# A frequency convolution whose odd chunk pairs hold their two halves swapped

## The chip, the core and the metric

The kernel runs on one core of a Trainium2 chip. The core has five engines that run at the same time and wait for each other through semaphores: TensorE (PE, matrix products), VectorE (DVE), ScalarE (ACT), GpSimd (POOL), and SyncE (SP, which here only issues DMA transfers). TensorE is an array of 128 x 128 cells. A product whose contraction has at most 64 rows, or whose result has at most 64 partitions, uses only a part of the array, and products on different parts can run side by side. Results of products go to PSUM, which has eight banks of 512 float32 per partition. Everything here is float32.

The metric is the device time of one execution in microseconds (us), lower is better.

## The reference, cut to what matters

The input x is (4, 512, 128, 64): batch B, time T, f, h. There are two layers. Layer 0 works on D = 128 * 64 = 8192 features per time step:

```
xn = layernorm(x over D);  k = xn @ Wk;  v = xn @ Wv;  r = sigmoid(xn @ Wr)     # D_STATE = 64
s_t = decay * s_(t-1) + k_t * v_t
x  = x + (r * s) @ Wo
xn = layernorm(x over D)
fo = conv over f, three taps, mixing all 64 h:  fo[f] = sum over d in -1, 0, 1 of freq_W[d] @ xn[f + d]
x  = x + gelu(fo + freq_b)
xn = layernorm(x over D);  to = depthwise causal conv over time, three taps;  x = x + layernorm(to)
x  = x + gelu(x @ W1 + b1) @ W2 + b2                                            # per (b, t, f): 64 -> 256 -> 64
```

Layer 1 takes a moving average over time as the trend, a Fourier transform of the rest over time, mixes its 128 lowest modes by one complex matrix per h, transforms back and adds the trend. The change touches layer 0 only; layer 1 reads what layer 0 leaves in DRAM.

The convolution over f is the place of the change. With 64 h per f, a chunk of 128 partitions holds two neighbouring f. One product of 128 x 128 covers what the two f of a chunk give to themselves and to each other. What is left are the two neighbours outside the chunk: the f before its first and the f after its second. Each of these is a product of 64 x 64.

## The kernel before, in words

The features lie on the partitions and time on the free axis: 64 chunks of (128, 512), handled in 32 pairs of chunks. For each batch layer 0 has stages, each a Python generator that writes instructions and yields after each step:

- `project(b)`: k, v and r for each pair, from loads of x (`xp`), of the weights and (batches 1 to 3) of x in rows for the statistics. Its TensorE line is L327; L324 scales the weights on VectorE.
- `scan(b)`: statistics, the recurrence, the gates; a chain of small steps.
- `attend_and_convolve(b)`: for each pair, `attend` (product with Wo, L453; sum with x, L455; scaling, L459, which gives `z`), and two pairs later `convolve`, then the column sums for the next layer norm (`add_up`, L215).
- `convolve_time(b)`: the causal convolution (VectorE lines L546, L548, L555) and again `add_up`.
- `open_feed(b)` and `feed_forward(b)`: the last layer norm and the feed-forward of each chunk: `widen` (L605), ScalarE's gelu (L609), `narrow` (L616, L621), and `store`: four transposes (L630) into one bank `pt`, a ScalarE copy of it into the row tile `ob` (L634), and a store to DRAM for every fourth chunk.

Before all that stands `project(0)`, and after it `prepare()`, which convolves the layer norm's scale and shift once (L153 to L163) for use as a correction inside the convolution (`cgr`, L474).

`convolve(i)` works on a PSUM tile `cv` of two banks, one for each chunk j of the pair. It issues four small products for the correction (L474), then the neighbours' products, then one full product for each chunk (L488); gelu, the sum (L491) and a square follow on ScalarE and VectorE. The neighbours' products of a pair are four: for each chunk one from the second half of the chunk before into the first half of this one, and one from the first half of the chunk after into the second half of this one:

```
if c > 0:
    nc.tensor.matmul(cv[0:H, j, :], lhsT=ws[c - 1][H:P, P:], rhs=zs[c - 1][H:P, :], ...)      # L481
if c < NCH - 1:
    nc.tensor.matmul(cv[H:P, j, :], lhsT=ws[c + 1][0:H, P:], rhs=zs[c + 1][0:H, :], ...)      # L484
```

So all L481 contract the rows 64 to 127 into the columns 0 to 63 of the array, and all L484 the rows 0 to 63 into the columns 64 to 127. `ws[c]` are the convolution's weights times the layer norm's scale of chunk c, made by ScalarE (L467).

The order: TensorE's instructions keep the order in which the code writes them. `in_turn` runs two generators side by side and takes steps from one or the other by given shares: `scan` and `attend_and_convolve` of batch 0 beside `project` and `scan` of batch 1; then `convolve_time(0)` beside `attend_and_convolve(1)`; then `feed_forward(0)` beside `project(2)`; and so on; near the end `feed_forward(2)` beside `convolve_time(3)`, and `feed_forward(3)` alone. On the other engines and DMA queues a scheduler orders the instructions by its own estimate of when each is ready; every engine and queue then runs its list in order. Buffers come from pools with a fixed number of copies, and a new use waits for the last reader of the old one. The PSUM pools have one copy each: a (two banks), c (two), m (two), s (one), p (one).

Of the kernel before, what the change touches and what calls it, by code (L numbers as in the profile page):

```python
# [12 lines left out]
ALU = mybir.AluOpType  # L13
# [3 lines left out]
P = 128  # L17
T = 512
NF = 128
H = 64  # L20
D = NF * H
NCH = D // P
SL = 512
NS = D // SL
NPR = NCH // 2
NT = T // P
S = 64
# [3 lines left out]
HALO = KMA // 2  # L31

MODES = np.concatenate([np.arange(0, M, 2), np.arange(1, M, 2)])
EPS = 1e-5


G1, B1, G2, B2, G3, B3, TB, G4, B4, W0, W1, W2 = range(12)
# [33 lines left out]

@with_exitstack
def layer0(ctx, tc, dram, x, xt, vecs, wkvr, wo, wdec, wconv, fbias, w1, fb1, w2, fb2, x4):


    nc = tc.nc
# [17 lines left out]
    def two(pool, tag):  # L94
        return pool.tile([P, 2, SL], F32, tag=tag, name=tag)
# [48 lines left out]
    tb_all = const.tile([P, NCH], F32, name="tb_all")  # L144
    fix = const.tile([P, NCH, 2], F32, name="fix")

    def prepare():

        both = rowp.tile([P, SL], F32, tag="rg", name="both")[:, 0:P].rearrange("p (k c) -> p k c", k=2)
        pc = two(ps_c, "c")  # L150
        for k, v in ((0, G2), (1, B2)):
            o = pc[:, k, :]
            nc.tensor.matmul(o[:, 0:NCH], lhsT=wc_sb[:, 0:P], rhs=vec[:, v, :], start=True, stop=True)  # L153
            nc.tensor.matmul(
                o[0:H, 1:NCH], lhsT=wc_sb[H:P, P:], rhs=vec[H:P, v, 0 : NCH - 1], start=False, stop=True,
                skip_group_check=True,
            )
            nc.tensor.matmul(
                o[H:P, 0 : NCH - 1], lhsT=wc_sb[0:H, P:], rhs=vec[0:H, v, 1:NCH], start=False, stop=True,
                skip_group_check=True,  # L160
            )
        nc.vector.tensor_scalar_mul(both[:, 0, :], pc[:, 0, 0:NCH], -1.0)
        nc.vector.tensor_scalar(both[:, 1, :], pc[:, 1, 0:NCH], fb_sb, None, ALU.add)  # L163
        pg = two(ps_c, "c")
        nc.tensor.transpose(pg[:, 0, 0:P], both.rearrange("p k c -> p (k c)"), ident)
        cgt = rowp.tile([P, SL], F32, tag="state", name="cgt")[:, 0:P]
        nc.vector.tensor_copy(cgt, pg[:, 0, 0:P])
        for k in range(2):
            nc.scalar.dma_start(cgd[:, k, :], cgt[k * NCH : (k + 1) * NCH, :])
# [267 lines left out]
    def attend_and_convolve(b):  # L437
# [23 lines left out]
        def scaled(i):  # L461

            wcs = fr.tile([P, 2, P + H], F32, tag="wcs", name="wcs")
            for j in range(2):
                c = 2 * i + j
                ws[c] = wcs[:, j, :]
                nc.scalar.mul(wcs[:, j, :], wc_sb, vec[:, G2, c : c + 1])  # L467

        def convolve(i):
            cv = c_bank() if i % 2 or held[0] else two(ps_m, "m")  # L470
            for h in range(2):
                for j in range(2):
                    q = 32 * (2 * h + j)
                    nc.tensor.matmul(  # L474
                        cv[h * H : (h + 1) * H, j, :], lhsT=cgr[q : q + 2, i, :], rhs=mb[q : q + 2, :],
                        start=True, stop=False,
                    )
            for j in range(2):
                c = 2 * i + j
                if c > 0:  # L480
                    nc.tensor.matmul(cv[0:H, j, :], lhsT=ws[c - 1][H:P, P:], rhs=zs[c - 1][H:P, :], start=False,  # L481
                                     stop=False)
                if c < NCH - 1:
                    nc.tensor.matmul(cv[H:P, j, :], lhsT=ws[c + 1][0:H, P:], rhs=zs[c + 1][0:H, :], start=False,  # L484
                                     stop=False)
            for j in range(2):
                c = 2 * i + j
                nc.tensor.matmul(cv[:, j, :], lhsT=ws[c][:, 0:P], rhs=zs[c], start=False, stop=True)  # L488
            nc.scalar.activation(cv, cv, AF.Gelu_apprx_tanh)
            x2 = two(bk, "x2")  # L490
            nc.vector.tensor_tensor(x2, cv, x1s.pop(i), ALU.add)  # L491
            nc.gpsimd.dma_start(x2d[b][2 * i : 2 * i + 2].rearrange("c p t -> p c t"), x2)
            sq2 = bk.tile([P, 2, SL], F32, tag="sq", name="sq2")
            nc.scalar.activation(sq2, x2, AF.Square)  # L494
            for c in (2 * i - 2, 2 * i - 1):
                zs.pop(c, None)
                ws.pop(c, None)
            if i + 2 < NPR:
                scaled(i + 2)
            waiting[i] = x2, sq2  # L500
# [95 lines left out]
    def feed_forward(b):  # L596
# [28 lines left out]
        def store(c):  # L625
# [5 lines left out]
            s = c // 4  # L631
            if c % 4 == 0:
                obs[s] = bk.tile([P, NT, SL], F32, tag="ob", name="ob")
            nc.scalar.copy(obs[s][:, :, c % 4 * P : (c % 4 + 1) * P], pt)  # L634
            if c % 4 == 3:
                nc.gpsimd.dma_start(
                    x4[b][:, s * SL : (s + 1) * SL].rearrange("(t p) d -> p t d", p=P), obs.pop(s)
# [292 lines left out]
def _inputs(x, i):  # L930


    def cols(v):
        return v.reshape(NCH, P).T

    time_w = i["time_W"].reshape(D, 3)
    vecs = [i[n] for n in ("ln_attn_g", "ln_attn_b", "ln_freq_g", "ln_freq_b", "ln_time_g")]
    vecs += [i[n] for n in ("ln_time_b", "time_b", "time_ln_g", "time_ln_b")]
    vecs += [time_w[:, k] for k in range(3)]
    wkvr = np.concatenate([i["Wk"], i["Wv"], i["Wr"], i["Wo"].T], axis=1)  # L940
    wo = i["Wo"].reshape(S, NPR, 2, P).transpose(2, 0, 1, 3)
    taps = i["freq_W"].transpose(2, 1, 0)
    wconv = np.zeros((P, 3 * H), np.float32)
    for a in range(2):
        for b in range(2):
            wconv[a * H : (a + 1) * H, b * H : (b + 1) * H] = taps[a - b + 1]
    wconv[H:, 2 * H :] = taps[0]
    wconv[:H, 2 * H :] = taps[2]
    b = x.shape[0]
    a = {  # L950
        "x": x.reshape(b, T, D),
        "xt": x.reshape(b, T, D).transpose(0, 2, 1).reshape(b, NCH, P, T),
        "vecs": np.stack([cols(v) for v in vecs], axis=1),
        "wkvr": wkvr.reshape(NCH, P, 4 * S),
        "wo": wo.reshape(P, NPR, P),
        "wdec": np.concatenate([i["w_decay"]] * 2)[:, None],
        "wconv": wconv,
# [26 lines left out]
```

## Time and profile before

| what | value |
|---|---|
| time, median of 3 runs | 4107.79 us (4098.11 to 4113.56) |
| time of the profiled execution | 4118.44 us |
| its span, first to last instruction | 4116.7 us |
| TensorE busy / granted clock, mean | 3908.1 us (95%) / 0.972 |
| VectorE busy | 2493.7 us (61%) |
| ScalarE busy | 1796.8 us (44%) |
| GpSimd busy | 527.2 us (13%) |

By stage (busy us of the engines within each stretch of the span):

| stretch, us | what runs | TensorE | VectorE | ScalarE | clock | DMA GB/s |
|---|---|---|---|---|---|---|
| 0 to 186 | `project(0)` | 180.9 | 25.8 | 38.0 | 1.00 | 155 |
| 186 to 262 | `prepare`, `scan(0)`, `project(1)` | 64.8 | 36.2 | 6.5 | 0.89 | 210 |
| 262 to 583 | `attend_and_convolve(0)` beside `project(1)`, `scan(1)` | 311.8 | 162.9 | 98.4 | 0.97 | 200 |
| 583 to 873 | `convolve_time(0)` beside `attend_and_convolve(1)` | 272.9 | 267.6 | 165.0 | 0.97 | 239 |
| 873 to 1298 | `feed_forward(0)` beside `project(2)` | 413.2 | 232.0 | 226.2 | 0.98 | 215 |
| 1298 to 1586 | `convolve_time(1)` beside `attend_and_convolve(2)` | 273.7 | 269.9 | 164.0 | 0.97 | 243 |
| 1586 to 2013 | `feed_forward(1)` beside `project(3)` | 415.5 | 225.8 | 224.8 | 0.98 | 212 |
| 2013 to 2309 | `convolve_time(2)` beside `attend_and_convolve(3)` | 275.9 | 268.6 | 164.6 | 0.94 | 239 |
| 2309 to 2600 | `feed_forward(2)` beside `convolve_time(3)` | 249.9 | 278.0 | 232.1 | 0.96 | 241 |
| 2600 to 2972 | `feed_forward(3)` | 365.3 | 202.9 | 276.2 | 0.99 | 161 |
| 2972 to 4116 | layer 1 | 1084.1 | 523.9 | 201.0 | 0.97 | 207 |

How to read the profile's lines: an engine is busy while an instruction of its own runs; waits and the issue of transfers are not counted. A group of instructions is given as line, engine, operation, output <- inputs, shape and count, then the busy time of the group (overlaps counted once), the mean duration in ns, and the idle time of the engine just before such instructions with what ended it. Products overlap in TensorE's pipeline, so their mean duration is longer than their spacing, and a float32 product is recorded as two instructions. Some records of products can be missing. The clock is the share of full speed that TensorE was granted.

### The profile page before, as it was taken

The numbers are of one execution on the slowest core, as the hardware profiler recorded it, in microseconds if no ns is written. First come the engines' busy times: TensorE is split into PE (matmuls) and PEld (weight loads), VectorE is DVE, ScalarE is ACT, GpSimd is POOL, SyncE is SP. The second block draws the span as 40 slices with busy tenths as digits, with TensorE's granted clock in tenths as the row PEclk, the third lists the DMA queues.
The fourth block names the chain that finished last, engine by engine and source line by source line (L and its number), as shares of the span: only waits on it lengthen the run. The fifth ranks groups of instructions, "written<-read, shape, count | busy, mean of one in ns | idle before, by whom it ended". The sixth has DMA issues, their size and how long they took to land. (4 is left out here: it accounts for less than half of the span.)

```text
span 4116.7 us, 46561 instructions
## 1 busy us (share of the span) xinstructions
PE 3908.1 (95%) x16939; PEld 1460.7 (35%) x16939; DVE 2493.7 (61%) x3168; ACT 1796.8 (44%) x2396; POOL 527.2 (13%) x942
## 2 busy tenths in 40 slices
PE   9999989999999999999999888999899999999998
PEld 4433322233333223333322322333325733228433
DVE  1145549975556997555699899655443355542555
ACT  2112336545555554555565678777622211122111
POOL 0000012310000221000122122000032000130000
PEclk9989999999999999999999999999999999999999
DMA  5466647776664776666477676555385377882577
GB/s 170 157 209 235 208 132 250 252 246 228 238 224 152 240 258 237 222 234 231 157 249 250 217 251 238 187 168 184 133 254 168 95 258 243 272 245 72 186 241 239
DMA packets 445854, 867.80 MB, mean 211 GB/s; under 512 B 35321, under 2 KB 101561, under 8 KB 445625
## 3 DMA queue, kind: packets, MB, share of 16 engines
q1 hardware_dynamic: 347136, 588.34, 44.6%
q0 software_dynamic: 62464, 207.66, 14.4%
q10 hardware_dynamic: 36024, 68.82, 4.5%
q8 instruction: 135, 2.21, 0.2%
q14 instruction: 95, 0.77, 0.1%
HBM read 596.18 MB, written 268.50 MB: 210 GB/s over the span
## 5 line engine op out<-in xcount | busy, mean ns | idle before, releaser
L616 PE MATMUL pa<-mid,w_sb 128*64 128x512 f32 x2048 | 499.7, 609 | 43.0 <-DVE x4t L621 42.6
L609 ACT ACTIVATE mid<-m,fb_sb 128x1024 f32<-128x1024 f32 x256 | 285.0, 1113 | 303.4 <-PE m L605 303.0
L621 DVE SCALAR_TENSOR_TENSOR x4t<-pa,fb_sb,x 128x512 f32<-128x512 f32 x252 | 188.0, 746 | 263.2 <-PE pa L616 263.2
L605 PE MATMUL m<-x,w_sb 64*128 64x512 f32 x1008 | 290.8, 650 | 5.7 <-ACT mid L609 5.2
L555 DVE SCALAR_TENSOR_TENSOR to<-xh,vec,to 128x512 f32<-128x512 f32 x384 | 277.0, 744 | 12.6 <-issue 8.6
L609 ACT ACTIVATE mid<-c,fb_sb 128x1024 f32<-128x1024 f32 x256 | 283.3, 1107 | 1.4 <-PE c L605 1.2
L845 ACT COPY even<-a 128x512 f32<-128x512 f32 x128 | 71.7, 588 | 480.3 <-PE b L865 145.8
L865 PE MATMUL b<-xin,avg_sb 128*128 128x512 f32 x512 | 246.6, 626 | 35.5 <-DMA xin<-x 32.4
L605 PE MATMUL c<-x,w_sb 64*128 64x512 f32 x1008 | 264.5, 598 | 0.7 <-ACT mid L609 0.7
L616 PEld LDWEIGHTS pa<-mid,w_sb 128*64 128x64 f32 x2048 | 124.8, 136 | 387.7 <-issue 229.8
L780 DVE TENSOR_TENSOR uv<-xin 128x1024 f32<-128x1024 f32 x128 | 151.2, 1222 | 172.4 <-PE a L791 135.7
L327 PE MATMUL a<-xp,both 128*128 128x512 f32 x512 | 247.5, 610 | 6.4 <-DVE both L324 5.9
L848 DVE TENSOR_TENSOR pm<-even,a 128x512 f32<-128x512 f32 x256 | 159.3, 683 | 143.5 <-ACT even L845 109.7
L791 PE MATMUL a<-uv,dft_sb 128*64 128x512 f32 x1024 | 241.2, 612 | 0.0
L840 PE MATMUL a<-xf,idft_sb 64*128 64x512 f32 x1024 | 239.8, 602 | 0.6 <-DVE pm L848 0.4
L871 DVE TENSOR_TENSOR xin<-b,pm 128x512 f32<-128x512 f32 x256 | 159.1, 684 | 116.4 <-PE b L868 116.4
L634 ACT COPY ob<-pt 128x512 f32<-128x512 f32 x256 | 148.9, 582 | 165.5 <-PE pt L630 165.2
L324 DVE TENSOR_SCALAR both<-both,vec 128x192 f32<-128x192 f32 x192 | 53.2, 316 | 251.9 <-DMA both<-in_wkvr 220.6
L796 ACT COPY xf<-a 128x512 f32<-128x512 f32 x128 | 80.9, 632 | 266.1 <-PE a L791 266.1
L215 PE MATMUL st<-x,ones 128*32 128x512 f32 x512 | 182.4, 615 | 14.3 <-DVE x L491 14.3
L582 ACT ACTIVATE kd<-kd,vec 128x512 f32<-128x512 f32 x256 | 193.5, 809 | 4.3 <-DVE kd L574 4.2
L494 ACT ACTIVATE sq<-x 128x1024 f32<-128x1024 f32 x128 | 134.6, 1052 | 117.7 <-DVE x L491 117.4
(234 smaller groups left out, 6879.3 us busy)
## 6 DMA issues: line engine op xcount, KB each, us to landing
xp<-in_xt SPq DMA_DIRECT2D x256, 512.0 KB
xin<-x SPq DMA_DIRECT2D x128, 1024.0 KB
kx<-x SPq DMA_DIRECT2D x224, 512.0 KB
x<-x POOLq DMA_DIRECT2D x128, 512.0 KB, 4.2
kh<-to SPq DMA_DIRECT2D x128, 512.0 KB
x<-ob POOLq DMA_DIRECT2D x64, 1024.0 KB, 6.6
out<-xin ACTq DMA_DIRECT2D x64, 1024.0 KB
both<-in_x SPq DMA_DIRECT2D x96, 512.0 KB
```

Source lines behind the costliest of these rows:

```text
L215: nc.tensor.matmul(st[32 * q : 32 * q + 32, :], lhsT=ones, rhs=src[:, j, :], start=first, stop=last,)
L327: nc.tensor.matmul(pa[:, k, :], lhsT=wq[:, j, k * P : (k + 1) * P], rhs=xp[:, j, :], start=first and j == 0, stop=last and j == 1,)
L555: nc.vector.scalar_tensor_tensor(to[:, j, :], xh[:, j, k : SL + k], vec[:, w, c], to[:, j, :], ALU.mult, ALU.add)
L582: tc.keep_in_program_order(nc.scalar.activation(d[:, j, :], d[:, j, :], AF.Identity, bias=vec[:, B4, c], scale=vec[:, G4, c]))
L605: nc.tensor.matmul(pm[:, h, :], lhsT=w1_sb[hs, m * P : (m + 1) * P], rhs=x3[hs, :], start=True, stop=True)
L609: nc.scalar.activation(mid, pm, AF.Gelu_apprx_tanh, bias=fb1_sb[:, m : m + 1])
L616: nc.tensor.matmul(pa[h * H : (h + 1) * H, :], lhsT=w2_sb[:, m, :], rhs=mid[:, h, :], start=(m == 0), stop=(m == 1),)
L621: nc.vector.scalar_tensor_tensor(x4t, pa, fb2_sb, x3s[c // 2][:, c % 2, :], ALU.add, ALU.add)
L791: nc.tensor.matmul(pf[r][h * H : (h + 1) * H, :], lhsT=dft_sb[:, h, i, r, :], rhs=uv[h][:, i, :], start=False, stop=(i == 1),)
L840: nc.tensor.matmul(eo[h], lhsT=idft_sb[hs, r, i, :], rhs=xf[hs, r, c], start=(r == 0), stop=(r == 1),)
L848: nc.vector.tensor_tensor(pm[:, k, :], even, eo[1], op)
L865: nc.tensor.matmul(po[j], lhsT=avg_sb[:, j, :], rhs=xin[:, j, :], start=True, stop=False)
```

## The change

In every second pair of chunks (the odd pairs) the two f of each chunk change places: partitions 0 to 63 hold the second f and 64 to 127 the first. All that lies along the features follows on the host: the transposed x, the vectors, the projection weights, Wo. The convolution's weights exist twice, for even and for odd pairs (q = 0 and 1), and `scaled` takes the one of its pair. The neighbours' products are found by two small functions. They are still four per pair, and each falls on another quarter: for an even pair, chunk j = 0 takes both its neighbours from the rows 0 to 63 and chunk j = 1 both from the rows 64 to 127; for an odd pair it is the other way round; and the two products of a chunk go to the two column halves.

`prepare` does its small convolution by chunk number modulo 4, with results in two PSUM tiles (pools c and m) instead of one. `store` puts the halves of an odd pair's chunk back in their places: its copy out of PSUM is two copies of 64 columns per transpose instead of one of 128.

```diff
+HALVES = np.arange(D).reshape(-1, 2, 2, 2, H)
+HALVES[:, 1] = HALVES[:, 1, :, ::-1].copy()
+HALVES = HALVES.reshape(D)
...
+    halves = [slice(0, H), slice(H, P)]
+
+    def neighbours(q, c):
+
+        return (c - 1, q), (c + 1, 1 - q)
+
+    def rows_of(q, d):
+
+        return 1 - q if d < 0 else q
+
     def prepare():
...
-        pc = two(ps_c, "c")
+
+        pcs = two(ps_c, "c"), two(ps_m, "m")
         for k, v in ((0, G2), (1, B2)):
-            o = pc[:, k, :]
-            nc.tensor.matmul(o[:, 0:NCH], lhsT=wc_sb[:, 0:P], rhs=vec[:, v, :], start=True, stop=True)
-            nc.tensor.matmul(
-                o[0:H, 1:NCH], lhsT=wc_sb[H:P, P:], rhs=vec[H:P, v, 0 : NCH - 1], start=False, stop=True,
-                skip_group_check=True,
-            )
-            nc.tensor.matmul(
-                o[H:P, 0 : NCH - 1], lhsT=wc_sb[0:H, P:], rhs=vec[0:H, v, 1:NCH], start=False, stop=True,
-                skip_group_check=True,
-            )
-        nc.vector.tensor_scalar_mul(both[:, 0, :], pc[:, 0, 0:NCH], -1.0)
-        nc.vector.tensor_scalar(both[:, 1, :], pc[:, 1, 0:NCH], fb_sb, None, ALU.add)
+            for r in range(2):
+                for q in range(2):
+                    j = r if q == 0 else 1 - r
+                    o, src = pcs[r][:, k, 0:NCH], vec[:, v, :]
+                    at = slice(2 * q + j, NCH, 4)
+                    nc.tensor.matmul(
+                        o[:, at], lhsT=wc_sb[:, q, 0:P], rhs=src[:, at], start=q == 0, stop=True,
+                        skip_group_check=True,
+                    )
+                for q in range(2):
+                    j = r if q == 0 else 1 - r
+                    for d, n in neighbours(q, 0):
...
+                        nc.tensor.matmul(
+                            pcs[r][halves[n], k, first : last + 1 : 4], lhsT=wc_sb[rs, qn, P:],
+                            rhs=vec[rs, v, first + d : last + d + 1 : 4], start=False, stop=True,
+                            skip_group_check=True,
+                        )
+        for r in range(2):
+            for q in range(2):
+                at = slice(2 * q + (r if q == 0 else 1 - r), NCH, 4)
+                nc.vector.tensor_scalar_mul(both[:, 0, at], pcs[r][:, 0, at], -1.0)
+                nc.vector.tensor_scalar(both[:, 1, at], pcs[r][:, 1, at], fb_sb, None, ALU.add)
...
-                nc.scalar.mul(wcs[:, j, :], wc_sb, vec[:, G2, c : c + 1])
+                nc.scalar.mul(wcs[:, j, :], wc_sb[:, i % 2, :], vec[:, G2, c : c + 1])
...
             for j in range(2):
                 c = 2 * i + j
-                if c > 0:
-                    nc.tensor.matmul(cv[0:H, j, :], lhsT=ws[c - 1][H:P, P:], rhs=zs[c - 1][H:P, :], start=False,
-                                     stop=False)
-                if c < NCH - 1:
-                    nc.tensor.matmul(cv[H:P, j, :], lhsT=ws[c + 1][0:H, P:], rhs=zs[c + 1][0:H, :], start=False,
-                                     stop=False)
+                for n, h in neighbours(i % 2, c):
+                    if 0 <= n < NCH:
+                        rs = halves[rows_of(n // 2 % 2, n - c)]
+                        nc.tensor.matmul(
+                            cv[halves[h], j, :], lhsT=ws[n][rs, P:], rhs=zs[n][rs, :], start=False, stop=False
+                        )
...
-            nc.scalar.copy(obs[s][:, :, c % 4 * P : (c % 4 + 1) * P], pt)
+            o = obs[s][:, :, c % 4 * P : (c % 4 + 1) * P]
+            if c // 2 % 2:
+                for h in range(2):
+                    nc.scalar.copy(o[:, :, halves[1 - h]], pt[:, :, halves[h]])
+            else:
+                nc.scalar.copy(o, pt)
...
-        return v.reshape(NCH, P).T
+        return v[HALVES].reshape(NCH, P).T
...
-    wo = i["Wo"].reshape(S, NPR, 2, P).transpose(2, 0, 1, 3)
+    wo = i["Wo"][:, HALVES].reshape(S, NPR, 2, P).transpose(2, 0, 1, 3)
...
-    wconv = np.zeros((P, 3 * H), np.float32)
...
+    wconv = np.zeros((P, 2, 3 * H), np.float32)
...
-        "xt": x.reshape(b, T, D).transpose(0, 2, 1).reshape(b, NCH, P, T),
+        "xt": x.reshape(b, T, D).transpose(0, 2, 1)[:, HALVES].reshape(b, NCH, P, T),
...
-        "wkvr": wkvr.reshape(NCH, P, 4 * S),
+        "wkvr": wkvr[HALVES].reshape(NCH, P, 4 * S),
```

More of the change, by code (lines that the diff above doesn't have):

```diff
@@ L162, in prepare @@
-        nc.vector.tensor_scalar_mul(both[:, 0, :], pc[:, 0, 0:NCH], -1.0)
-        nc.vector.tensor_scalar(both[:, 1, :], pc[:, 1, 0:NCH], fb_sb, None, ALU.add)
+            for r in range(2):
[10 more added lines that the diff above has]
+                    for d, n in neighbours(q, 0):
+                        first, last = 2 * q + j, 2 * q + j + NCH - 4
+                        first, last = first + 4 * (first + d < 0), last - 4 * (last + d >= NCH)
+                        qn = (first + d) // 2 % 2
+                        rs = halves[rows_of(qn, d)]
+                        nc.tensor.matmul(
[3 more added lines that the diff above has]
+                        )
@@ L940, in _inputs @@
     wkvr = np.concatenate([i["Wk"], i["Wv"], i["Wr"], i["Wo"].T], axis=1)
-    wo = i["Wo"].reshape(S, NPR, 2, P).transpose(2, 0, 1, 3)
+    wo = i["Wo"][:, HALVES].reshape(S, NPR, 2, P).transpose(2, 0, 1, 3)
     taps = i["freq_W"].transpose(2, 1, 0)
-    wconv = np.zeros((P, 3 * H), np.float32)
[L944 to L948, printed above, removed]
+    wconv = np.zeros((P, 2, 3 * H), np.float32)
+    for q in range(2):
+        for a in range(2):
+            sa = slice((a ^ q) * H, (a ^ q) * H + H)
+            for b in range(2):
+                wconv[sa, q, (b ^ q) * H : (b ^ q) * H + H] = taps[a - b + 1]
+            wconv[sa, q, 2 * H :] = taps[2 - 2 * a]
     b = x.shape[0]
```

## The prediction

> **What bounds the kernel now.** I read the slices of the span first, then the busy time of each engine in stretches of 40 us, then the order of time inside one pair, then the groups of instructions by line. The slices say that TensorE is over 90% busy almost everywhere, and that VectorE is too in three places:
>
> ```profile
> PE   9999989999999999999999888999899999999998
> DVE  1145549975556997555699899655443355542555
> ```
>
> The change makes TensorE's work shorter only in `attend_and_convolve`, so what it is worth depends on who is the bound where that function runs. It runs four times: batch 0 beside `project` of batch 1 (262 to 583 us), and batches 1, 2 and 3 beside `convolve_time` of the batch before (583 to 873, 1298 to 1586 and 2013 to 2309 us). One stretch of each (columns: window, then busy us and instruction count of TensorE, weight loads, VectorE, ScalarE, GpSimd; granted clock, DMA share, GB/s):
>
> ```profile
> 400.00:440.00 40.00, 40.00 (x158) 12.33 (x156) 22.01 (x27) 11.45 (x17) 2.91 (x4) 1.00 0.70 230
> 680.00:720.00 40.00, 38.47 (x182) 9.80 (x182) 39.29 (x44) 23.95 (x32) 11.52 (x23) 1.00 0.76 252
> 1480.00:1520.00 40.00, 38.75 (x184) 10.36 (x184) 39.86 (x43) 24.89 (x35) 11.70 (x20) 1.00 0.77 264
> 2120.00:2160.00 40.00, 37.96 (x184) 10.02 (x182) 39.08 (x44) 23.68 (x32) 10.01 (x19) 0.96 0.74 249
> ```
>
> In the first, TensorE has no gap and VectorE is half idle. In the other three VectorE is 98 to 99.7% busy: it is the bound, and TensorE's 95% is no sign of the contrary. The same follows from the groups between 560 and 900 us:
>
> ```profile
> L555 DVE SCALAR_TENSOR_TENSOR to<-xh,vec,to 128x512 f32<-128x512 f32 x128 | 93.2, 743 | 2.5 <-ACT to L551 1.3 <-issue 0.8
> L459 DVE TENSOR_TENSOR z<-x,rm 128x1024 f32<-128x1024 f32 x32 | 39.0, 1218 | 0.2
> L455 DVE TENSOR_TENSOR x<-a,xp 128x1024 f32<-128x1024 f32 x32 | 39.0, 1217 | 1.6 <-PE a L453 1.4
> L546 DVE TENSOR_TENSOR kd<-kx,rm 128x1024 f32<-128x1024 f32 x32 | 38.7, 1216 | 0.5 <-ACT rm L249 0.5
> L548 DVE TENSOR_TENSOR xh<-kd,rm 128x1024 f32<-128x1024 f32 x32 | 38.7, 1216 | 0.0
> ```
>
> A pair of chunks costs VectorE 4 x 0.743 + 5 x 1.22 = 9.1 us there (fifth operation: L491). TensorE's work per pair is 7.7 to 7.8 us, the spacing where nothing stalls (705.54 to 713.32). Now one pair's convolution on TensorE, in order of time (start, us, line):
>
> ```profile
> 705.54 1.09 PE L474 MATMUL m<-rm,cgr 2*64 2x512 f32 x8
> 706.55 0.64 PE L481 MATMUL m<-z,wcs 64*64 64x512 f32 x1
> 707.03 0.59 PE L481 MATMUL m<-z,wcs 64*64 64x512 f32 x1
> 707.46 0.59 PE L481 MATMUL m<-z,wcs 64*64 64x512 f32 x1
> 707.89 0.59 PE L481 MATMUL m<-z,wcs 64*64 64x512 f32 x1
> 708.42 1.98 PE L488 MATMUL m<-z,wcs 128*128 128x512 f32 x4
> ```
>
> A float32 product leaves two records. Each L481 has its L484 10 ns behind it, on the opposite quarter, so four products take four steps, 706.55 to 708.42 = 1.87 us. The four of L474, on four tiles of the array, take 1.01 us. Layer 1 has the very pattern that the change makes: two row groups times two column halves, each row group with a bank of its own.
>
> ```profile
> 3006.26 1.09 PE L787 MATMUL a<-edge,dfte_sb 24*64 24x512 f32 x8
> 3007.28 3.65 PE L791 MATMUL a<-uv,dft_sb 128*64 128x512 f32 x16
> ```
>
> Eight records, four products, 1.02 us.
>
> **What the Trainium skill says.** "TensorEngine Tiling (Array Packing)", "Tile-to-Partition Mapping", gives 64x64 mode four tiles, and "Key Properties" says that tiles work in parallel and that a change of mode drains the engine: L787 agrees on the first, and the number of mode changes per pair stays the same. "PSUM Pressure" there says that different row tiles may not use one PSUM bank at a time: in the changed code chunk j of a pair uses one row half alone and bank j, so this holds, as in L787. "TensorE: Matmul & The Clock Gate", "What overlaps and what doesn't", lets a weight load overlap only where the row group differs; the new order has two neighbours on one row half. L787's order has that too and loses nothing, so the trace decides. Part 1 of that page says an idle window of about 3.4 us halves the clock; here 3.05 us of idle at 785 us was enough, with products at half rate after it.
>
> **The change part by part.**
> 1. Neighbour products. 1.87 becomes about 1.02 us, 0.855 us less per pair; 128 pairs, 109 us of TensorE work. (The end pairs of a batch have three products: two rounds before, one after, the same gain.)
> 2. Batch 0, TensorE-bound: of 32 pairs one stands in the stall at 521 to 526 us, where TensorE waits for the scan of batch 1. 31 x 0.855 = 26.5 us. Cover: the tightest feed is `project`'s weights, issued at 404.76, scaled by 409.5, used at 412.91. This leaves 3.4 us, and 2.5 after. DMA goes from 228 GB/s to about 248; other stretches move 264.
> 3. Batches 1 to 3, VectorE-bound: between their first and last VectorE instruction VectorE is idle 22.0, 17.2 and 26.2 us, 65 in all, and no gain can exceed that, though 82 us of TensorE work go. The idle time lies at the heads (before VectorE saturates: 7, 5 and 4 convolutions) and the tails (2, 2 and 4). These 24 x 0.855 = 20.5 us are the most that I can place; part of each head is a chain of ScalarE and GpSimd that doesn't shrink. I take 12 us, ends 0 and 30 (a half of the idle time).
> 4. `prepare`: 6 small products become 24, on two banks. Now 186.12 to 187.34, 1.22 us: 0.31 per full product, 0.06 to 0.12 per quarter. After: 8 x 0.31 + 16 x 0.1 = 4.1, so +2.9; VectorE's 2 evacuations become 8 at about 0.12 (+0.6), and TensorE stands behind them at L165 and then in `project` of batch 1, whose bank m is now borrowed. Nothing covers it: +3.5 us, ends 1 and 6.
> 5. Evacuation of the transposes (L634): 128 of 256 copies become two of 256 elements. From 0.582 us for 512 and 1.052 for 1024 elements (L494), about 0.35 each by itself; two issue closer than that (L582: 0.81 each, two in 1.51). So +0.03 to +0.12, and at most +0.30, from L467's 0.44 for 192. I take +0.12, 15 us of ScalarE in all. Cover: ScalarE is idle 47% beside `project`, 20% in 2309 to 2600, 26% in 2600 to 2972; the transposes into this bank come again only after 4.3 us or more, and `narrow` takes mids made a chunk before. On the path: +1 us, ends 0 and 5. Without the cover: 15 to 38.
> 6. The scale of the weights reads one of two matrices: same shape, same 0.44 us. Loading 98 KB more at the start: at 155 GB/s 0.6 us, behind other loads, 0. Host-side reordering: outside the time.
> 7. Order. In the built program TensorE's list differs in `prepare` alone. The scheduler swaps a few neighbours on VectorE, ScalarE, GpSimd's queue (7 moved lines) and SP's (7), in short runs inside the three stages and at the start of the next. `kx` and `xp` loads change places by one or two; one such issue is about 0.5 us and SP waits in order. No view prices this: +-5 us, taken as 0.
>
> Sum: -26.5 - 12 + 3.5 + 1 = -34 us. The profiled execution took 4118.44 us (span 4116.7), 10.65 above the median 4107.79; the stages are the same, so I take the sum off the median: 4074 us. A measurement of this kernel can tell about 0.5%, 20.5 us, from no change.
>
> **Rivals.**
> A. All TensorE work counts: -109 + 4.5, 4003 us; or, with VectorE's idle time used up, -26.5 - 65 + 4.5, 4021. For it: TensorE is 93% busy there. Against: 9.1 us of VectorE per pair.
> B. Nothing in the three stages, and the higher ends of 4, 5 and 7: -26.5 + 6 + 5 + 5 = -10.5, 4097 us.
> C. The quarters don't run four at a time: +3.5 + 1, 4112 us. Against: L787. For: its halves stream the same data, ours different ones, and its rows number 24, not 64.
> D. Slower: in the three stages TensorE now waits about 2.1 us per pair, not 1.3, and drops to half clock. The stall at 521 us shows the price: the pair at 530 took 11.29 us in place of 6.85, 4.4 more. Eight such drops that VectorE's backlog doesn't cover undo the 34 us; with twelve it is 4074 + 53 = 4127 us. Against: 2400 to 2600 us, with TensorE 85 to 91% busy, runs at clock 1.00, as its waits are short.
>
> **How the numbers follow.** Forecast 0.66, its own range 4056 to 4087. A 0.07, B 0.16, C 0.05, D 0.06. Low end: the forecast with 30 us in item 3 and 1 in item 4 is 4053; part of A moves it to 4046. High end: past B, 4100; that leaves C, D and most of A out, 0.16. Faster by over 0.5% (under 4087): forecast, A and a third of B, 0.78; within: the rest of B and most of C, 0.15; slower: D and the last of C, 0.07.
>
> **What would show it.** Right: L481's successor has four starts within 0.05 us and a group takes 1.0 us; the spacing of batch 0's pairs drops from 10.48 to about 9.6; VectorE stays at 98% in the middle of the three stages and TensorE falls to about 85%; layer 1 keeps its 1144 us; the stages from 873 and 1586 keep theirs within 3 us. Wrong: groups of 1.9 us (C), clock under 0.9 in the three stages (D), or these stages 20 us shorter each (A).

## The result, and the profile after

| | before | after |
|---|---|---|
| time, median | 4107.79 us (4098.11 to 4119.38) | 4080.06 us (4069.98 to 4089.58) |
| ratio | | 0.9927, interval 0.9898 to 0.9956 |
| profiled execution, span | 4116.7 us | 4087.8 us |
| TensorE / VectorE / ScalarE busy | 3908.1 / 2493.7 / 1796.8 us | 3830.4 / 2493.8 / 1802.8 us |

The change saves 27.7 us by the medians and 28.9 us by the two profiled spans; 34 were predicted. The same kernel, timed once more for the later experiments, gave a ratio of 0.9914 (0.9900 to 0.9928), some 35 us.

The order of time inside a pair of batch 0, after (start, us, line; L505 was L474, L514 was L481 and L484, L519 was L488):

```profile
401.23 1.09 PE L505 MATMUL c<-rm,cgr 2*64 2x512 f32 x8
402.25 1.09 PE L514 MATMUL c<-z,wcs 64*64 64x512 f32 x8
403.26 1.98 PE L519 MATMUL c<-z,wcs 128*128 128x512 f32 x4
```

The eight records of four neighbour products now stand in one line, because they start together: 402.25 to 403.26, 1.01 us in place of 1.87.

The stretches of 40 us, one of batch 0 and one of each of the three stages beside `convolve_time` (window; busy us and count of TensorE, weight loads, VectorE, ScalarE, GpSimd; clock, DMA share, GB/s):

```profile
400.00:440.00 40.00, 40.00 (x178) 12.37 (x178) 23.85 (x30) 11.90 (x18) 3.07 (x5) 1.00 0.78 257
680.00:720.00 40.00, 36.67 (x184) 8.72 (x188) 39.19 (x44) 25.43 (x35) 10.14 (x20) 0.96 0.74 244
1460.00:1500.00 40.00, 37.58 (x190) 8.95 (x188) 39.86 (x43) 23.71 (x32) 12.20 (x20) 1.00 0.77 265
2100.00:2140.00 40.00, 36.68 (x186) 8.92 (x180) 39.08 (x43) 24.01 (x32) 10.02 (x19) 0.90 0.73 247
```

TensorE still has no gap in batch 0. In the other three VectorE is as full as before, and TensorE has fallen only from 95 to 97% to 92 to 94% although its work per pair fell by 0.855 us in 9.1: it waits in short pieces, and in two of the three the granted clock is lower (0.96 and 0.90). VectorE's work there is what it was:

```profile
L586 DVE SCALAR_TENSOR_TENSOR to<-xh,vec,to 128x512 f32<-128x512 f32 x128 | 93.3, 744 | 3.3 <-issue 1.6 <-ACT to L582 1.3
L579 DVE TENSOR_TENSOR xh<-kd,rm 128x1024 f32<-128x1024 f32 x32 | 38.7, 1218 | 0.0
```

Where the 28.9 us went, from the starts and ends of the stages in the two traces:

| stretch | before, us | after, us | gain |
|---|---|---|---|
| start to the first correction product of batch 0 | 261.9 | 266.4 | -4.5 |
| from there to the first VectorE operation of `convolve_time(0)` | 349.2 | 329.0 | +20.2 |
| `convolve_time(0)`, (1), (2) beside the next batch's convolution (the third up to the last sum `x2` of batch 3) | 261.3, 285.9, 294.8 | 262.5, 281.0, 288.2 | -1.2, +4.9, +6.6 |
| the two feed-forward stages between them | 425.7, 429.2 | 427.0, 430.2 | -1.3, -1.0 |
| `feed_forward(2)` beside `convolve_time(3)`, to the end of the latter | 303.1 | 297.2 | +5.9 |
| the rest, layer 1 included | 1505.6 | 1506.2 | -0.6 |

Batch 0 gave 6.3 us less than the 26.5 predicted. Its pairs now start every 9.64 us, as expected, but four of them outside the stall of the scan took 10.53, 11.23, 11.35 and 11.29 us. TensorE's waits between 266 and 480 us (columns: total us, times, longest) show one kind, which the kernel before does not have there:

```profile
PE c L505 <- DVE x L522: 2.7, 2, 1.6
```

The order of time around the first of them, of TensorE and VectorE:

```profile
309.88 0.55 DVE L355 TENSOR_SCALAR both<-both,vec 128x192 f32<-128x192 f32 x2 [2.77 <-DMA both<-in_wkvr]
...
312.57 1.29 DVE L352 BATCH_NORM_STATS2 stt<-both 128x6 f32<-128x512 f32 x2 [2.14 <-DMA both<-in_x]
312.89 1.13 PE L484 MATMUL a<-rst,wo_sb 64*128 64x512 f32 x4
313.78 1.21 DVE L522 TENSOR_TENSOR x<-c,x 128x1024 f32<-128x1024 f32 x1
315.04 1.09 PE L505 MATMUL c<-rm,cgr 2*64 2x512 f32 x8 [1.02 <-DVE x L522]
...
316.06 1.99 PE L514 MATMUL c<-z,wcs 64*64 64x512 f32 x8
...
317.97 2.68 PE L519 MATMUL c<-z,wcs 128*128 128x512 f32 x4
```

Read from the end: the products write the tile c, which comes free with the sum `x2` (L522) of the pair before. That sum is VectorE work, and in VectorE's list it stands behind `project`'s `bn_stats` (L352), which waits 2.14 us for rows of `in_x`, issued at 304.45 and not there before 312.5. So a load that no product uses holds TensorE up for 1.02 us, and the products after it run at half speed (1.99 and 2.68 us in place of 1.09 and 1.98). In batch 0 c is the only tile for this, since m is held by `project(1)`.

### The profile page after: what moved, and what is told of

It reads as the page before. It is cut to its first block, busy times and chain, and to the rows that moved or that the text cites. A ratio compares the mean times of both kernels' runs of the same rounds, so it can differ in the third digit from the quotient of the medians.

```text
span 4087.8 us, 46889 instructions
## 1 busy us (share of the span) xinstructions
PE 3830.4 (94%) x16975; PEld 1425.9 (35%) x16975; DVE 2493.8 (61%) x3174; ACT 1802.8 (44%) x2524; POOL 527.7 (13%) x942
## 5 line engine op out<-in xcount | busy, mean ns | idle before, releaser
L586 DVE SCALAR_TENSOR_TENSOR to<-xh,vec,to 128x512 f32<-128x512 f32 x384 | 276.9, 745 | 10.8 <-issue 6.8
L246 PE MATMUL st<-x,ones 128*32 128x512 f32 x512 | 205.8, 618 | 35.7 <-DVE x L522 35.6
L246 PE MATMUL st<-sq,ones 128*32 128x512 f32 x640 | 173.4, 619 | 21.1 <-ACT sq L525 20.0
```

The lines of the kernel that those rows point to most:

```text
L246: nc.tensor.matmul(st[32 * q : 32 * q + 32, :], lhsT=ones, rhs=src[:, j, :], start=first, stop=last,)
L586: nc.vector.scalar_tensor_tensor(to[:, j, :], xh[:, j, k : SL + k], vec[:, w, c], to[:, j, :], ALU.mult, ALU.add)
```

## The experiments

**Where the saved TensorE time counts.** The first three runs take the four-at-a-time order away, in batches 1 to 3, in batch 0, and in all. The layout stays; each chunk's full product is issued between the two groups of neighbours, so that a group holds two products. For batches 1 to 3:

```diff
                 for n, h in neighbours(i % 2, c):
                     ...
+                if not (b == 0):
+                    nc.tensor.matmul(cv[:, j, :], lhsT=ws[c][:, 0:P], rhs=zs[c], start=False, stop=True)
-            for j in range(2):
+            for j in range(2 if b == 0 else 0):
                 c = 2 * i + j
                 nc.tensor.matmul(cv[:, j, :], lhsT=ws[c][:, 0:P], rhs=zs[c], start=False, stop=True)
```

> The changed kernel, but in batches 1 to 3 the four neighbours' products are issued as two and two, with a full product between, so that only batch 0 has rounds of four. Theory (VectorE bounds the three stages with batches 1 to 3, TensorE bounds batch 0): batch 0's pairs keep their 9.64 us spacing, the three stages grow by no more than 11 to 16 us in all, 4091 to 4096 us. Rival (the gain is spread evenly over the 128 pairs, three quarters of it in batches 1 to 3): 4080 + 21 = 4101 us.

Measured: 4100.97 us, ratio 0.9982 (0.9967 to 0.9996).

The same with batch 0 in place of the others:

```diff
-                if not (b == 0):
+                if not (b > 0):
-            for j in range(2 if b == 0 else 0):
+            for j in range(2 if b > 0 else 0):
```

> The changed kernel, but batch 0 issues its neighbours' products as two and two, so that only batches 1 to 3 have rounds of four. Theory: batch 0's pairs go back to 10.5 us and its stage grows by about 20 us, 4098 to 4102 us. Rival (even spread): a quarter of 28, 4080 + 7 = 4087 us.

Measured: 4120.57 us, ratio 1.0036 (1.0021 to 1.0050).

And in all batches:

```diff
-                if not (b > 0):
+                if not (False):
-            for j in range(2 if b > 0 else 0):
+            for j in range(2 if False else 0):
```

> The changed kernel with the products as two and two in every batch: new layout, new small convolution at the start, split copies, but no rounds of four. Theory (the rounds of four are the whole gain, the rest costs 4 to 8 us): 4112 to 4116 us, that is 0 to 0.2% above the kernel before. Rival (a good part of the gain comes from the changed order on VectorE and the queues): 4095 us or less.

Measured: 4144.75 us, ratio 1.0093 (1.0063 to 1.0123), slower than the kernel before. All three lie above what was expected, and the first even at the rival's 4101, because this way of undoing is dearer than the old order. The order of time in the last of them:

```profile
406.55 1.08 PE L514 MATMUL c<-z,wcs 64*64 64x512 f32 x4
407.56 1.13 PE L518 MATMUL c<-z,wcs 128*128 128x512 f32 x2
408.61 1.08 PE L514 MATMUL c<-z,wcs 64*64 64x512 f32 x4
409.62 1.12 PE L518 MATMUL c<-z,wcs 128*128 128x512 f32 x2
410.58 1.88 PE L358 MATMUL m<-xp,both 128*128 128x512 f32 x4
```

From the first neighbour to the end of the full products it is 4.03 us. In the kernel before it is 3.69, in the changed one 2.84. So undoing costs 1.19 us per pair: 0.855 us for the pairing, and 0.33 us more, put down here to the two further changes between quarter and full products. This was not allowed for in the expectations.

With that size the runs can still be compared with each other. Against 4080.06 us, undoing batch 0 costs 40.5 us for 32 pairs, 1.27 us each, all of the 1.19 and a little more. Undoing the other three costs 20.9 us for 96 pairs, 0.22 us each. Both cost 64.7 us, about the sum, 61.4. A quarter of the pairs carries two thirds of the time: TensorE's saving counts in full in batch 0 and for about a fifth in the others. An even spread over the pairs, the rival, would have put about 15 us into batch 0, and falls. Against the second timing of the changed kernel, with ratio 0.9914, the two costs would be about 50 and 28 us, and batch 0 still carries nearly two thirds.

The starts of pairs in batch 1 show which fifth. The microseconds from one pair's first product to the next one's, from the first pair of the batch on (572.92 and 568.60 us), worked out from the two traces:

```
changed kernel              7.81  6.01 11.13 6.01 6.24 10.03 7.88 9.85 8.52 9.45 9.59
two-and-two, batches 1-3   11.73 12.35 13.91 7.20 7.20  8.05 8.05 8.69 8.51 9.45 9.59
```

At the head, where VectorE is not yet full, the kernel goes at TensorE's pace: 6.01 became 7.20, and the first three spacings together 13 us longer (the granted clock from 500 to 620 us is 0.79 there, 0.87 in the changed kernel). From the ninth spacing to the last of the batch both took 205.6 us, the same to within 0.01: there both go at VectorE's pace. In batch 3's stage the undoing cost more than in the two others (303.3 us against 288.2; 284.2 against 281.0 and 263.0 against 262.5), so there the longer products did reach the bound.

**Is VectorE the bound there?** The multiplication L577 moves to GpSimd:

```diff
-                nc.vector.tensor_tensor(xr, x2, pair_of(rb), ALU.mult)
+                nc.gpsimd.tensor_tensor(xr, x2, pair_of(rb), ALU.mult)
```

> The changed kernel with one of VectorE's nine operations per pair of the causal convolution stage (x2 times the row, 1.22 us) done by GpSimd. Theory: VectorE's 9.1 us per pair become 7.9, still above TensorE's 6.9, so the three stages and the one at 2286 us shrink, each of the three by up to 38 us (3965 us in all) as long as GpSimd does it in under 7.9 us and doesn't slow VectorE; if it takes longer, GpSimd is the bound and the stages grow. Rival (DMA or TensorE bounds the stages): no shorter than 4080 us although VectorE's busy share falls.

Measured: 4197.63 us, ratio 1.0219 (1.0192 to 1.0246). Slower, since the work that stayed on VectorE grew. VectorE's groups from 640 to 760 us, first of the changed kernel, then of this one, and GpSimd's of this one:

```profile
L586 DVE SCALAR_TENSOR_TENSOR to<-xh,vec,to 128x512 f32<-128x512 f32 x58 | 42.5, 744 | 0.9 <-issue 0.8
L579 DVE TENSOR_TENSOR xh<-kd,rm 128x1024 f32<-128x1024 f32 x16 | 19.5, 1217 | 0.0
```

```profile
L586 DVE SCALAR_TENSOR_TENSOR to<-xh,vec,to 128x512 f32<-128x512 f32 x52 | 62.6, 1212 | 0.4
L579 DVE TENSOR_TENSOR xh<-kd,rm 128x1024 f32<-128x1024 f32 x13 | 18.0, 1387 | 1.1
L490 DVE TENSOR_TENSOR z<-x,rm 128x1024 f32<-128x1024 f32 x13 | 15.8, 1217 | 0.0
```

```profile
L577 POOL TENSOR_TENSOR kd<-kx,rm 128x1024 f32<-128x1024 f32 x13 | 28.5, 2194 | 0.8 <-DVE xh L579 0.5
```

VectorE lost one operation of 1.22 us per pair and got 4 x 0.468 + 0.17 = 2.04 us back, about as long as GpSimd's one operation. The means hide how. The order of time of VectorE and GpSimd in one pair (the 3.59 us are two operations, the first of 2.80):

```profile
662.04 1.22 DVE L522 TENSOR_TENSOR x<-c,x 128x1024 f32<-128x1024 f32 x1
663.18 3.59 DVE L586 SCALAR_TENSOR_TENSOR to<-xh,vec,to 128x512 f32<-128x512 f32 x2
663.23 2.19 POOL L577 TENSOR_TENSOR kd<-kx,rm 128x1024 f32<-128x1024 f32 x1
667.82 0.74 DVE L586 SCALAR_TENSOR_TENSOR to<-xh,vec,to 128x512 f32<-128x512 f32 x1
```

Of the 52 L586, the 12 beside which L577 ran took 2.77 us in the mean, and the other 40 took 0.75 as before. "SBUF — State Buffer", section "SBUF: two separate sides", in the Trainium skill says that VectorE operations with two SBUF inputs and GpSimd's that read SBUF share a port pair as an exclusive lock; L586 and L579 have two such inputs, and the trace agrees. L490 has two as well and kept its 1217 ns only because it never ran beside L577 in these 120 us: where it did, as at 1397.96 us, it took 1.94 us. L486 and L522 take one input from PSUM, and beside L577 they kept their 1.22 us (15 and 5 times up to 2700 us). The pair now costs VectorE 9.9 us, not 9.1: 0.8 x 32 = 26 us per stage. From the first to the last L586 of a stage it became 282.1 us from 255.6 and 281.6 from 261.2. VectorE stayed at 98.7% of these 120 us and TensorE fell from 90.6% to 82.9%. The time followed VectorE; the expected direction was wrong, and the bound was confirmed by it.

**Why batch 0 fell short.** The theory is the wait read above: `bn_stats` waits for a load, and the sum and the tile c wait behind it. Four kernels on one chip, the changed one first:

> The changed kernel once more, as the yardstick for the three runs beside it. Both theories: 4080 us within 5. In its profile TensorE waits in batch 0 (266 to 480 us) about 2 to 3 us in all at the correction product for the sum x2 (L522 on VectorE), and two to four pairs take 11 us or more in place of 9.64.

Measured: 4072.52 us, ratio 0.9914 (0.9900 to 0.9928); four waits for the sum in batch 0, 3.1 us; four pairs of 10.55 to 11.36 us.

```diff
-                    nc.vector.bn_stats(stt[:, h + t, s, :], xk[:, t, :])
+                    nc.vector.bn_stats(stt[:, h + t, s, :], xp[:, t, :])
```

> The bn_stats of project read xp in place of the rows of in_x, so that the statistics are computed from other data and the output differs; VectorE does the same work, but no longer waits there for the load of in_x. Theory (the bank of the products comes free late, because the sum x2 stands on VectorE behind a bn_stats that waits for in_x): the wait of the correction product for x2 in batch 0 goes to 0, the stretched pairs outside the stall at 513 us come back to 9.64 us, about 6 us less in that stage and 4074 us in all. Rival (the stretched pairs have another cause, the clock or the loads themselves): they stay above 11 us and the time stays at 4080 within 2.

Measured: 4089.99 us, ratio 0.9949 (0.9934 to 0.9964). Slower: `xp` lands later still, and `bn_stats` now waits for that (3.28, 3.31 and 4.53 us between 320 and 346 us). TensorE's waits of this kernel from 266 to 500 us, to be set beside the line of the changed kernel above:

```profile
PE c L505 <- DVE x L522: 8.4, 10, 1.6
```

Neither expectation held: it was not the absence of a wait but a longer one. Ten waits in place of two, and eight pairs of 10.02 to 11.29 us, speak for the theory; the experiment had not isolated what it was meant to. (This kernel leaves out the true statistics of batches 1 to 3, and so do the two with resident data below; batch 0's own data stay what they were.)

The load of `in_x` moved ahead of the weights' and `xp`'s in the code:

```diff
+                    nc.sync.dma_start(xk, x[b, h * P : (h + 2) * P, ...])
             nc.sync.dma_start(wq[:, :, 0 : 4 * S], wkvr[2 * i : 2 * i + 2].rearrange("c p s -> p c s"))
             xp = load_x(b, i)
...
-                nc.sync.dma_start(xk, x[b, h * P : (h + 2) * P, ...])
```

> In project, the load of in_x is issued ahead of the pair's weights and of xp, about 1.5 us earlier; all computation is the same. Theory: bn_stats no longer waits last, but the scale of the weights (L355), which stands right behind it on VectorE and ahead of x2's sum as often, waits for a load that is now issued later; so the wait moves by one instruction and the time is 4077 to 4083. If in_x alone was the late one, 4074 as in the run with statistics of xp.

Measured: 4095.43 us, ratio 0.9957 (0.9943 to 0.9970), above the expectation. VectorE's waits between 262 and 490 us, two lines of the changed kernel and two of this one:

```profile
DVE both L355 <- DMA both<-in_wkvr: 32.9, 17, 4.1
DVE stt L352 <- DMA both<-in_x: 28.5, 18, 3.0
```

```profile
DVE stt L353 <- DMA both<-in_x: 53.0, 20, 5.5
DVE both L356 <- DMA both<-in_wkvr: 3.7, 6, 0.8
```

The wait moved by one instruction and hardly shrank, but in the opposite direction to the one expected: from the weights' scale to `bn_stats`. The pairs up to the stall were not the place of the loss: 24 of their spacings took 222.24 us, against 223.89 in the changed kernel run beside it. Lost were 8.1 us ahead of batch 0's first pair and 12.0 and 8.1 us in the two feed-forward stages beside `project` (434.6 and 433.6 us); that was not foreseen, and its cause was not traced.

`bn_stats` written after the pair's products:

```diff
-                for t in range(2):
-                    nc.vector.bn_stats(stt[:, h + t, s, :], xk[:, t, :])
...
+                if b > 0 and j == 1:
+                    for t in range(2):
+                        nc.vector.bn_stats(stt[:, h + t, s, :], xk[:, t, :])
                 yield 1.0
```

> In project of batches 1 to 3, the two bn_stats are written after the pair's products; all computation is the same. On VectorE the sum x2 then comes before the bn_stats in about half of the pairs of batch 0 and after it in the rest. Theory: half or more of the stretched pairs come back, 3 to 6 us less, 4074 to 4077. Rival (stretch has another cause): 4080 within 2.

Measured: 4068.93 us, ratio 0.9895 (0.9881 to 0.9909). Two of the stretched pairs were gone (at 303 to 326 us), but VectorE's list still had `bn_stats` ahead of the sum there; the rows had come sooner before the pair. This run doesn't tell the two apart, and its ratio is not clearly below the changed kernel's.

The clean form reads resident data, the decays, so that no load can hold `bn_stats`:

```diff
-                    nc.vector.bn_stats(stt[:, h + t, s, :], xk[:, t, :])
+                    nc.vector.bn_stats(stt[:, h + t, s, :], decb[:, 0:SL])
```

> The bn_stats of project read a resident row of decays in place of the rows of in_x, so that the statistics are computed from other data and the output differs; VectorE does the same work and all loads are made, but bn_stats waits for no load at all. Theory (x2's sum is held up on VectorE behind a bn_stats that waits for a load): the pairs stretched to over 11 us before the scan's stall come back, except where the scale of the weights (L355), which also waits for a load, stands ahead of the sum; ratio to the kernel before 0.988 to 0.990, that is 5 to 10 us under the changed kernel. Rival (loads or the clock as such): stretched pairs remain and the ratio is 0.991 to 0.993, as for the changed kernel.

Measured: 4059.56 us, ratio 0.9876 (0.9859 to 0.9893), at or a little below the expectation. From 261 to 480 us TensorE has no wait at all, and a pair at about the same time runs at full speed:

```profile
319.13 1.09 PE L505 MATMUL c<-rm,cgr 2*64 2x512 f32 x8
...
320.15 1.09 PE L514 MATMUL c<-z,wcs 64*64 64x512 f32 x8
...
321.17 1.98 PE L519 MATMUL c<-z,wcs 128*128 128x512 f32 x4
```

Up to the stall no spacing but the first is over 9.64 us. In the profiles it is 12.5 us faster than the changed kernel run beside the others, all of it by the first operation of `convolve_time(0)`: 2.6 us ahead of the first pair, 7.0 in the pairs up to the stall, 3.5 in and after the stall.

A kernel that computes the right statistics and gives the rows a pair of time more, with `bn_stats` at the head of the next pair:

```diff
             first, last = i == 0, i == NPR - 1
+            if b > 0 and i > 0:
+                for t in range(2):
+                    nc.vector.bn_stats(stt[:, h + t, s, :], xk[:, t, :])
...
-                for t in range(2):
-                    nc.vector.bn_stats(stt[:, h + t, s, :], xk[:, t, :])
...
         if b == 0:
             add_up(st, *waiting, False, True)
+        else:
+            for t in range(2):
+                nc.vector.bn_stats(stt[:, h + t, s, :], xk[:, t, :])
```

> In project of batches 1 to 3, the two bn_stats of a pair are written at the head of the next pair; all computation is the same. The rows of in_x have then had a whole pair of time to land, but their buffer comes free a few us later. Theory: no wait of the correction product for x2 in batch 0, as with the resident data, ratio 0.988 to 0.990; if the later release of the buffer delays the next pair's loads, the weights become the late ones and the ratio is 0.991 to 0.994. Rival (loads or the clock as such): 0.991 to 0.993 with the stretched pairs where they were.

Measured: 4070.34 us, ratio 0.9907 (0.9894 to 0.9921): no clear gain over the changed kernel, although the 24 spacings ahead of the stall fell to 219.72 us. Three waits for the sum stayed in batch 0, 2.4 us. Ahead of the first stand the weights' scale, which waited 3.79 us for its weights, and a `bn_stats` that waited 0.74 us more for `in_x`, ahead of the second the weights' scale, which waited 3.14 us for its weights, and ahead of the third, at 458.84 us, the `bn_stats` of the batch's last pair, which has no next pair, with the aggregation behind it:

```profile
458.84 1.29 DVE L368 BATCH_NORM_STATS2 stt<-both 128x6 f32<-128x512 f32 x2 [2.03 <-DMA both<-in_x]
460.05 1.02 DVE L395 BATCH_NORM_AGGREGATE mv<-stt 128x2 f32<-128x96 f32 x2
...
461.58 1.22 DVE L526 TENSOR_TENSOR x<-c,x 128x1024 f32<-128x1024 f32 x1
```

Last, the resident data in the kernel before the change, by the same edit of `bn_stats` (its L321):

> The kernel before the change, with bn_stats reading the resident row of decays as in the run on the changed kernel (statistics from other data). It tells whether what the resident data gave there, 7 us between the first pair of batch 0 and the scan's stall, is a loss that the change brought, or one that the kernel had anyway. Theory (before the change no pair waits for x2, since a pair has 10.48 us): the pairs keep their 10.48 us and the span between the first pair and the last one ahead of the stall keeps its 252 us within 3; ratio 0.997 to 1.000. Rival (the waits for in_x cost both kernels the same): 7 us less there, ratio 0.995 to 0.997.

Measured: 4092.37 us, ratio 0.9957 (0.9943 to 0.9971). The places are the theory's and the ratio the rival's. From the second pair to the one ahead of the stall, 24 spacings, it took 237.44 us, and 237.64 without the edit: the loads of `in_x` cost these pairs nothing before the change, though `bn_stats` waited for them as long there (31.4 us between 262 and 490 us, 28.5 after the change). The 20 us that the profile gained lie elsewhere: 3.0 ahead of the first pair, 1.9 in that pair, and 6.0 and 10.3 in the two feed-forward stages beside `project`. Stages like these differ by 4 to 5 us between two runs of the changed kernel too (427.0 and 430.2 against 422.6 and 425.6), so the last two numbers are rough.

The two kernels with resident data show the change without this wait. The same 24 spacings took 237.44 us and 217.15: 0.845 us each, within 0.01 of the 0.855 predicted. Their medians differ by 32.8 us (0.9876 / 0.9957 = 0.9919). That is about what the change gave with the wait (0.9927 and 0.9914), so the whole times don't show the cost of the wait; the spacings do, and two profiles of the changed kernel agree on them (223.58 and 223.89 us).

One rival is left, that the scheduler put `bn_stats` ahead of the sum only in the changed kernel. The traces rule it out. From 192 to 602 us VectorE, ScalarE, GpSimd and SyncE have the same order of instructions in both kernels. The two-and-two run has the changed kernel's order on these four throughout, and there, at 10.83 us per pair, `bn_stats` waited 29.9 us for `in_x` between 262 and 500 us and TensorE not once for the sum. So it is the pace of the pairs that lets the wait reach TensorE.

## Why the prediction was right, step by step

1. Neighbour products: right. 1.01 us against 1.02, 0.86 less per pair. Two neighbours on one row half lost nothing, and 64 rows with different data went as layer 1's 24 rows did.
2. Batch 0: 20.2 us against 26.5. TensorE was the bound, and the spacing of 9.64 us was the predicted one; the failing step is the cover. The prediction took the weights as the tightest feed of a 9.6 us pair, with 2.5 us to spare. The tightest was on another engine: the rows for `bn_stats`, which gate VectorE's list and through it tile c. With 10.48 us per pair that chain was in time, with 9.64 it is late at times. The 24 spacings took 223.58 us, 6.43 more than with resident data, as much as the shortfall; outside them the first spacing gained 2.7 us too much and the end of the stretch 2.6 too little, which cancel by chance. Freed of the wait, the 24 spacings gain what was predicted.
3. Batches 1 to 3: 10.3 us against 12. The sizes differ by stage (-1.2, 4.9, 6.6), and the mechanism is the one given: VectorE is the bound. Its idle time from the first multiplication of each stage (L546, now L577) to the stage's end went from 8.2, 17.2 and 26.2 us to 9.3, 12.5 and 19.6, which is the gain to within 0.2 us. Most of it lies where VectorE is not full yet or no longer. But 2.7 us of the second stage's gain lie in the middle, between the ninth and the thirteenth pair: there VectorE's list has another order in the changed kernel, and the two-and-two run with that order has the same 2.0 us idle in place of 4.7. That part is the order's and not the products'. TensorE did not fall to about 85% busy but to 91% from 640 to 760 us (108.73 of 120). In the second stage, between the 14th and the 29th pair, its other products took 0.84 us less per pair (5.19 from 6.03), but the column sums (L246) 0.31 more (2.95 from 2.64). They now start in parts: at 1471.99 us two of their products ran alone for 1.04 us, and the rest from 1473.08 on.
4. `prepare`: 2.4 us against 3.5. From its first product to `project`'s next it was 186.12 to 188.19 and is 187.58 to 192.09. The table's 4.5 us hold 1.5 that came earlier; the first four runs of the experiments and the changed kernel again began batch 0 between 262.9 and 264.4 us, so the rest is variation.
5. Split copies: smaller than taken. ScalarE's total grew by 6.0 us, not 15; two half copies take 0.374 us each and 0.65 together, where one took 0.58. Stages in which they lie did not grow, and the path's +1 us can't be told from their variation.
6. Weights and loads at the start: nothing to be seen, as predicted.
7. Order: taken as 0 within 5. `feed_forward(2)` beside `convolve_time(3)` became about 6 us shorter, in the changed kernel (297.2 from 303.1), and as much in nine of the ten other runs with the new layout (296.7 to 298.2), the two-and-two ones among them. The old layout with resident data keeps 303.0. So it belongs to the layout and what the scheduler made of it, not to the products. VectorE's list has another order there, from 2329 us on; which move in it did it was not traced.

The sum was near partly by luck: 2, 3 and 4 were off by -6, -2 and +1, and the order, priced at nothing, gave +6 back. The rest, about 5 us lost, lies ahead of batch 0, in the feed-forward stages and in layer 1, and is within the variation between runs. The rivals: A falls, since the three stages stay with VectorE; B, with nothing in them, lies 17 us above, and undoing there costs 21 us; C falls with item 1. D's mechanism, a wait and then half clock, did occur. In batch 0 it is new, twice ahead of the stall. From the first to the last L586 of the three stages the clock fell to a half 11 times, for 61 us in all, against 8 times and 44 us before; in the second profile of the changed kernel it was 6 times and 40 us. Most of that was covered, since the three stages together became 10.3 and 9.4 us shorter.

D also shows that the length of one wait doesn't tell whether the clock falls. "TensorE: Matmul & The Clock Gate", Part 1, names an idle window of about 3.4 us before the clock halves; here the clock was 0.50 for 3.4 us after waits of 1.02 and 1.64 us (from 315.99 and 469.59 us), and stayed at 1.00 from 846 to 869 us in spite of this one:

```profile
852.41 1.04 PE L246 MATMUL st<-x,ones 128*32 128x512 f32 x2 [2.51 <-DVE x L522]
```

So the measurement decides, and it leaves open what else counts. The prediction's reason against D, that the waits from 2400 to 2600 us are short, was wrong: the longest there is 2.6 us, and the clock was 1.00.

## What to carry to other kernels

When the pace of a loop is raised, list every instruction that stands ahead of the buffer's release on each engine's list, and ask of each which load it waits for; the load that TensorE uses need not be the one that is late first. A saving on one engine is worth its full size only where no other engine's list is full, and the head of such a stage may still collect a part. An experiment that takes a wait away should read data that is already resident; other data that also arrives by a load only moves the wait.

## What was not expected of the hardware

- In batch 0 a TensorE wait of only 1.02 or 1.64 us was followed by 3.4 us at half clock, so that the two spacings beside it took 2.7 and 3.4 us more (10.53 and 11.23 in place of 9.44 and 9.64; 11.35 and 11.29 in place of 9.64 twice). A wait of 2.51 us elsewhere had no such end.
- Going back and forth between quarter and full products cost about 0.17 us per change (4.03 - 2.84 - 0.86 = 0.33 us for two more in a pair).
- One 2.2 us multiplication on GpSimd per pair held the VectorE operation beside it by about 2.0 us where that one has both inputs in SBUF (L586: 2.77 us in place of 0.75), and not at all where one input comes from PSUM (L486 and L522: 1.22 us).
